# Deformable convolution layer: y offsets of two tap rows loaded onto all lanes, spread matmuls in three batches per row block

## The chip, the core and the metric

The kernel runs on one NeuronCore of a Trainium2 chip. The metric is the device time of one execution in microseconds. Before the change it is 5572.56 us, the median of 3 runs (5569.03 to 5573.76).

## What is computed

Four residual layers act on a 4 x 128 x 128 x 128 image (batch, height, width, channels). Only layer 0 is touched by the change. It is a group norm followed by a deformable 3 x 3 convolution with 4 groups of 32 channels, a ReLU and the residual. Cut to what matters:

```python
offset = einsum('bchw,oc->bohw', gn(x), w_off) + b_off     # 4 groups x 9 taps x (dy, dx)
py = off_y + (ky - 1) + row
px = off_x + (kx - 1) + column
val = bilinear(gn(x), py, px)        # four neighbours, zero outside the image
x = x + relu(einsum('bgckhw,ogck->bohw', val, w_def))
```

Bilinear sampling at (py, px) is the same as summing the pixels q near a place with weights max(0, 1 - |py - qy|) * max(0, 1 - |px - qx|). Each factor is called a tent here. As long as no offset is larger than 1 in size, nine taps around a block of pixels need only a window of pixels around the block; for other inputs a general version stands behind a test at the end of the layer.

## The kernel before, in words

All of it is in `deform_layer` (from L181). The image of each of the 4 batches is cut into 43 blocks of 3 rows (RY = 3), so 172 blocks are worked off in one loop (L699). Inside a block the columns are cut into 33 pieces of 4 columns (RX = 4). A piece of 3 x 4 outputs reads a window of 5 x 6 = 30 pixels; with 4 channel groups these are 120 lanes, the partitions on which most of the work lies.

The stages of a block are these.

1. `load_places` (L444) brings the offsets of a block into `places`: 24 partitions per set (4 groups, 6 parts each), where an offset is kept as three bf16 parts and the three parts of its positive half. Eight transfers on SP's queue per block, from the DRAM tiles `offs`. `load_pixels` (L462) brings the pixel windows, four transfers on SP's queue.
2. `spread_offsets` (L474, matmul L498) turns the offsets of a tap into tents on all 120 lanes with small bf16 matmuls of 25 rows: three of 130 columns for y (one per row of the block) and four of 99 columns for x. Taps are taken in the five slots of `SLOTS` (L50): four slots hold two taps, one holds one. The result lies in `t_ps`, a PSUM tile of two banks in a pool with two buffers.
3. `tents` (L504) multiplies the y tent by the x tent: ACT copies the y part to SBUF (`ty`, L508), DVE multiplies it by the x part in PSUM into `m` (L510). `m` exists twice, for this block and the next.
4. `sample` (L514, matmul L521) multiplies the pixels of a piece, as weights, by `m`, into `v_ps`; ACT copies the result to `v` (`keep_samples`, L528, copy L531).
5. `convolved` (L568, matmul L579) does the 3 x 3 convolution over `v` of this block and the one before, and DVE adds the residual (L552).

The order of the instructions on the five engines is that of the code: L680 asks for a manual schedule. In the loop over the blocks an inner loop of eight steps i (L709) does two things at once: `sample` for four pieces of this block, and the spread and tents of the next block, which `advance` and `DONE` (L650) lay into the steps i = 0, 2, 3, 5 and 6. Between them stand one third of the convolution of the block before, six statistics for the next norm (`count`), and one or two steps of `prepared` (L358), the job that makes the tables of pixels and offsets of later rows: transposes (L370), their copy with the norm (L373), the stores `tab<-rows` (L378, L380), the offset matmul (L385), the offsets (L390, L393), their splitting into parts (L409 to L418) and the store `off<-parts` (L423), once in eight rows.

Each transfer, on whichever queue, takes one of eight completion semaphores in turn. All transfers of the loop are issued by SP.

The loop's inner part, which sets the order on every engine:

```python
for i in range(NG_X):                                    # L709
    if i == 3:
        load_row(n + 2)
    todo = advance(NB_ * (n + 1) + DONE[i])
    if vps is not None:
        keep_samples(*vps)
    next(convs, None)
    vps = sample(m, pix, i, NK * RY), vk, i, NK * RY
    multiply(todo)
```

Of the kernel before, what the change touches and what calls it, by code (L numbers as in the profile page):

```python
# [49 lines left out]
SLOTS = [(0, 6), (1, 7), (2, 8), (3, 5), (4,)]  # L50
# [130 lines left out]
def deform_layer(tc, c, small, x, w_off, b_off, w_def, x1, tabs, offs):  # L181
# [13 lines left out]
    NB = RY * PADW  # L195
    with ExitStack() as ctx:
        wp = ctx.enter_context(tc.tile_pool(name="l0w", bufs=1))
        ps_g = ctx.enter_context(tc.tile_pool(name="l0ps_g", bufs=1, space=PSUM))
        ps_t = ctx.enter_context(tc.tile_pool(name="l0ps_t", bufs=2, space=PSUM))
# [4 lines left out]
        NPH = NPY + NPX  # L204
        keep = ctx.enter_context(tc.tile_pool(name="l0keep", bufs=2))
# [9 lines left out]
        places = [wp.tile([P, len(SLOTS), RY, OW], BF16, name=f"places_{i}") for i in range(3)]  # L215
        last = wp.tile([P, 3, 1, OW], BF16, name="places_last")
        pixels = [wp.tile([P, NXB + 1, P], F32, name=f"pixels_{i}") for i in range(2)]
        parts = wp.tile([2 * NL, NPART, 2 * RO * OW], BF16, name="parts")

        def rims():  # L220

            zero = two.tile([P, 2 * SX * P], F32, name="zero", tag="m")
            nc.vector.memset(zero, 0.0)
            zrow = zero[0 : NXB + 1]
            zoff = zero[0 : 2 * NL, 0 : NPART * OW].bitcast(BF16)
            zoff = zoff.rearrange("p (n l) -> p n l", n=NPART)
            for b in range(B):
# [14 lines left out]
                nc.scalar.dma_start(rows_[:, :, (S + 2) * OW :], zoff)  # L242

        def tables():

            awayi = two.tile([NG, NPH, LANES], I32, name="awayi", tag="x1c")
# [22 lines left out]
            for i, sign in enumerate((-1.0, 1.0, 1.0)):  # L269
                nc.gpsimd.memset(picks[:, i], sign)  # L270
# [17 lines left out]
            for t in (*pixels, parts):  # L288
                nc.gpsimd.memset(t, 0.0)
            yield  # L290
            picks16 = one.tile([NG, 3, P], BF16, name="picks16", tag="ve")
            nc.vector.tensor_copy(picks16, picks.rearrange("g k q r -> g k (q r)"))
            kinds = two.tile([NG, 3, NPH * LANES], BF16, name="kinds", tag="m")
# [10 lines left out]
            n = NPH * LANES // 3  # L304
            for h in range(3):
                if h % 2 == 0:
                    tp = ps_t.tile([P, 2, 512], F32, name="t_ps")
                at = slice(h * n, (h + 1) * n)
                for i in range(3):
                    nc.tensor.matmul(  # L310
                        tp[:, h % 2, 0:n], lhsT=picks16[:, i], rhs=kinds[:, i, at],
                        start=i == 0, stop=i == 2,
                    )
                nc.scalar.copy(to[:, at], tp[:, h % 2, 0:n])
# [43 lines left out]
        def prepared(b, y0):  # L358
# [6 lines left out]
            for h in range(0, RC, RO):  # L365
# [23 lines left out]
                off = one.tile([2 * NL, RO, S], F32, name="off")  # L389
# [8 lines left out]
                p0 = h % (2 * RO)  # L398
                at = slice(p0 * OW, (p0 + RO) * OW)

                def to(i):
                    return parts[:, i, at].rearrange("p (r c) -> p r c", c=OW)[:, :, 2 : S + 2]

                def high(t):
                    halves = t.rearrange("p r c -> p (r c)").bitcast(BF16)
                    return halves.rearrange("p (r c two) -> p r c two", r=RO, two=2)[:, :, :, 1]

                rest = one.tile([2 * NL, RO, S], F32, name="rest")
                nc.scalar.copy(to(0), high(off))  # L409
                nc.gpsimd.tensor_tensor(rest, off, high(off), ALU.subtract)  # L410
                flat = off.rearrange("p r c -> p (r c)")
                nc.vector.tensor_reduce(ranges[:, 0, n : n + 1], flat, AX.X, ALU.max)
                yield
                nc.vector.tensor_reduce(ranges[:, 1, n : n + 1], flat, AX.X, ALU.min)
                nc.scalar.copy(to(1), high(rest))
                nc.gpsimd.tensor_tensor(to(2), rest, high(rest), ALU.subtract)
                yield
                nc.vector.tensor_scalar(  # L418
                    parts[:, NSPLIT:, at], parts[:, 0:NSPLIT, at], 0.0, None, ALU.max
                )  # L420
                if p0:
                    r0 = y0 + h - p0 + 2
                    nc.sync.dma_start(  # L423
                        offs[b].rearrange("(p n) l -> p n l", n=NPART)[
                            :, :, r0 * OW : (r0 + 2 * RO) * OW
                        ],
                        parts,
                    )
                    ready[b] = y0 + h + RO
                    yield  # L430
                yield

        def shifted(b, d, k, n, row, count):

            ky, kx = divmod(k, 3)
            wide = (S + 4) * OW
            first = (d * NK + k) * NG * NPART
            whole = offs[b]
            return bass.AP(
                whole.tensor, whole.offset + first * wide + (row - ky + 2) * OW + 2 - kx,  # L440
                [[wide, NG * NPART], [NG * NPART * wide - 1, n], [1, count]],
            )

        def load_places(b, j):  # L444
            t = places[(b * NYB + j) % 3]
            for d in range(2):
                for q, slot, k, n in ((0, 0, 0, 3), (0, 3, 3, 2), (1, 0, 6, 3), (1, 3, 5, 1)):
                    p1 = 64 * d + 32 * q + 1
                    nc.sync.dma_start(
                        t[p1 : p1 + KROWS - 1, slot : slot + n].rearrange("p k r c -> p k (r c)"),  # L450
                        shifted(b, d, k, n, RY * j, RY * OW),
                    )
            if j + 1 == NYB:
                for d in range(2):
                    p1 = 64 * d + 33
                    nc.sync.dma_start(
                        last[p1 : p1 + KROWS - 1].rearrange("p k r c -> p k (r c)"),
                        shifted(b, d, 6, 3, PADW - 1, OW),
                    )
            return t  # L460
# [13 lines left out]
        def spread_offsets(src, slot, taps, rows):  # L474

            tps, todo = [], []
            for q in taps:
                tp = ps_t.tile([P, 2, 512], F32, name="t_ps")
                tps.append(tp)
                for d in range(2):  # L480
                    p0 = 64 * d + 32 * q
                    wide = OW if d else PADW
                    to = tp[0:LANES, d, 0 : rows * wide].rearrange("p (r c) -> p r c", c=wide)
                    mov = src[p0 : p0 + KROWS, slot]
                    if d == 0:
                        ph0 = 0 if rows == RY else RY
                        lot = [(ph0 + r, to[:, r], mov[:, r, 0:PADW]) for r in range(rows)]
                    else:
                        lot = []
                        for i in range(NPX):  # L490
                            cs = slice(i, OW, RX)
                            lot.append((NPY + i, to[:, :, cs], mov[:, :, cs]))
                    todo.append([(p0, *v) for v in lot])
            for i in range(max(map(len, todo))):
                for lot in todo:
                    if i < len(lot):
                        p0, ph, to, mov = lot[i]
                        nc.tensor.matmul(  # L498
                            to, lhsT=spread[p0 : p0 + KROWS, ph, :], rhs=mov,
                            start=True, stop=True,  # L500
                        )
            return tps

        def tents(tp, m, rows):  # L504

            n = rows * PADW
            ty = two.tile([LANES, NB], F32, name="ty")
            nc.scalar.copy(ty[:, 0:n], tp[0:LANES, 0, 0:n])  # L508
            tx = tp[0:LANES, 1, 0 : rows * OW].rearrange("p (r c) -> p r c", c=OW)[:, :, 0:PADW]
            nc.vector.tensor_tensor(  # L510
                m, ty[:, 0:n].rearrange("p (r c) -> p r c", c=PADW), tx, ALU.mult
            )
# [55 lines left out]
        def convolved(b, y0, y1, terms, stats, first, each):  # L568
# [7 lines left out]
            for m, ((ky, at, v, k0, r0, r1), kx) in enumerate(todo):  # L576
                if m >= first and (m - first) % each == 0:
# [3 lines left out]
                    rhs=v[:, k0 + kx, r0:r1, kx : kx + S],  # L581
# [66 lines left out]

        NB_ = len(SLOTS)
        DONE = [1, 1, 2, 3, 3, 4, 5, 5]  # L650
        assert len(DONE) == NG_X and DONE[-1] == NB_
        rows_in, ms = {}, {}
        made = [0]

        def advance(upto):

            todo = []
            while made[0] < min(upto, NB_ * len(blocks)):
                n, slot = divmod(made[0], NB_)
                taps = range(len(SLOTS[slot]))  # L660
                tps = spread_offsets(rows_in[n], slot, taps, RY)
                todo.extend((n, SLOTS[slot][q], tp) for q, tp in zip(taps, tps))
                made[0] += 1
            return todo

        def multiply(todo):
            for n, k, tp in todo:
                if n not in ms:
                    ms[n] = two.tile([LANES, NK, RY, PADW], F32, name="m")
                tents(tp, ms[n][:, k], RY)  # L670
# [7 lines left out]

        order = {getattr(mybir.EngineType, e) for e in ("PE", "Activation", "DVE", "Pool", "SP")}
        ctx.enter_context(tc.manual_schedule(engines=order))  # L680
        nc.scalar.dma_start(woff, w_off)
        nc.scalar.dma_start(boff, b_off.rearrange("o n -> n o"))
# [13 lines left out]
        for i in range(NB_):  # L696
            multiply(advance(i + 1))
# [1192 lines left out]
```

## Time and profile before

| what | value |
|---|---|
| median of the runs | 5572.56 us |
| the profiled execution, and its span | 5567.76 us, 5565.9 us |
| mean granted TensorE clock | 0.971 |
| PE busy in the span | 5163.0 us (93%) |
| DVE, ACT, POOL busy | 3079.9 (55%), 2721.1 (49%), 787.0 us (14%) |
| first and last sample matmul of the loop | 119.0 us, about 3304 us |
| SP's queue: packets, MB, share of 16 DMA engines | 1127664, 657.77, 45.2% |
| ACT's queue: packets, MB, share | 10182, 6.43, 0.4% |
| spread matmuls L498 | x10836 on `places`, x60 on `places_last` |
| sample matmuls L521 | x11352 on `m`, x264 on `me` |

The profile is of one execution. Busy time counts instructions at work, without waits; a group's line gives the busy time, the mean duration of one instruction, and the idle time of the engine before it with what ended it. Matmuls are pipelined, so their durations overlap; what one costs the engine is read from the starts of the timeline. The granted clock is the share of full speed that the throttle gave TensorE. The DMA share is the mean over the core's sixteen DMA engines.

### The profile page before, as it was taken

The numbers are of one execution on the slowest core, as the hardware profiler recorded it, in microseconds if no ns is written. First come the engines' busy times: TensorE is split into PE (matmuls) and PEld (weight loads), VectorE is DVE, ScalarE is ACT, GpSimd is POOL, SyncE is SP. The second block draws the span as 40 slices with busy tenths as digits, with TensorE's granted clock in tenths as the row PEclk, the third lists the DMA queues.
The fourth block names the chain that finished last, engine by engine and source line by source line (L and its number), as shares of the span: only waits on it lengthen the run. The fifth ranks groups of instructions, "written<-read, shape, count | busy, mean of one in ns | idle before, by whom it ended". The sixth has DMA issues, their size and how long they took to land. (4 is left out here: it accounts for less than half of the span.)

```text
span 5565.9 us, 112097 instructions
## 1 busy us (share of the span) xinstructions
PE 5163.0 (93%) x42401; PEld 4438.1 (80%) x42401; DVE 3079.9 (55%) x10450; ACT 2721.1 (49%) x5802; POOL 787.0 (14%) x698
## 2 busy tenths in 40 slices
PE   2899999999999999999999989999989889898896
PEld 1778888888888888888888878999967768577686
DVE  6544444554444644444433337888876574764844
ACT  1345555445554455554544432333345475664755
POOL 2021111001111011111100002222210010110102
PEclk9899999999999999999999989999989999999999
DMA  4555555555555555554543423233232352642525
GB/s 142 146 129 137 128 136 122 127 118 135 133 131 119 131 112 137 129 141 113 124 78 76 76 56 91 91 107 103 91 100 92 97 195 80 207 147 82 203 95 169
DMA packets 1138394, 671.46 MB, mean 121 GB/s; under 512 B 737133, under 2 KB 1003566, under 8 KB 1121206
## 3 DMA queue, kind: packets, MB, share of 16 engines
q1 hardware_dynamic: 1127664, 657.77, 45.2%
q8 instruction: 338, 5.54, 0.4%
q10 hardware_dynamic: 10182, 6.43, 0.4%
q14 instruction: 210, 1.72, 0.1%
HBM read 382.88 MB, written 281.11 MB: 119 GB/s over the span
## 5 line engine op out<-in xcount | busy, mean ns | idle before, releaser
L510 DVE TENSOR_TENSOR m<-ty,t_ps 120x390 f32<-120x390 f32 x1548 | 805.0, 557 | 1497.2 <-ACT ty L508 1496.0
L521 PEld LDWEIGHTS v_ps<-m,pixels 120*128 120x128 f32 x11352 | 1436.1, 194 | 86.0 <-issue 8.7
L521 PE MATMUL v_ps<-m,pixels 120*128 120x108 f32 (+1 forms) x11352 | 1462.3, 273 | 3.6 <-ACT v L531 3.5
L531 ACT COPY v<-v_ps 128x432 f32<-128x432 f32 x1376 | 719.7, 523 | 1268.7 <-PE v_ps L521 1265.8
L579 PE MATMUL conv_ps<-v,wdef 128*128 128x128 f32 (+2 forms) x5160 | 1301.8, 378 | 6.5 <-DVE x1c L552 5.9
L579 PEld LDWEIGHTS conv_ps<-v,wdef 128*128 128x128 f32 x5160 | 812.8, 192 | 256.0 <-issue 21.7
L508 ACT COPY ty<-t_ps 120x390 f32<-120x390 f32 x1560 | 688.2, 489 | 176.9 <-PE t_ps L498 169.5
L498 PE MATMUL t_ps<-places,spread 25*120 25x99 bf16 (+1 forms) x10836 | 520.0, 259 | 62.1 <-DVE m L510 37.8
L498 PEld LDWEIGHTS <-spread 25*120 25x120 bf16 x10896 | 338.9, 136 | 224.5 <-issue 124.6
L1639 PEld LDWEIGHTS proj_ps<-wcat,X 128*128 128x128 f32 x4096 | 473.2, 192 | 19.1 <-issue 18.9
L393 POOL TENSOR_TENSOR off<-off,koff 72x512 f32<-72x512 f32 x128 | 162.1, 1266 | 2294.1 <-DVE off L390 2215.8
L1639 PE MATMUL proj_ps<-wcat,X 128*128 128x128 f32 x4096 | 481.3, 276 | 0.0
L1072 ACT ACTIVATE rowT<-x1T_ps,t_x,s_x 128x128 f32<-128x128 f32 x512 | 192.7, 457 | 366.4 <-PE x1T_ps L1065 342.8
L1085 PE MATMUL m_ps<-carry,w 128*128 128x172 f32 x2286 | 361.5, 311 | 0.0
L1646 DVE TENSOR_TENSOR L<-proj_ps,work 128x256 f32<-128x256 f32 x256 | 108.6, 424 | 430.0 <-ACT work L1643 429.9
L1085 PEld LDWEIGHTS m_ps<-carry,w 128*128 128x128 f32 x2286 | 345.5, 188 | 0.0
L1185 POOL TENSOR_TENSOR sum_h<-sum_h,x2c 128x512 f32<-128x512 f32 x128 | 163.2, 1275 | 1159.4 <-DVE x2c L1145 1159.4
L1736 POOL TENSOR_TENSOR gate<-normed,gate 128x512 f32<-128x512 f32 x128 | 163.4, 1276 | 1127.8 <-ACT normed L1735 867.2
L1643 ACT ACTIVATE work<-proj_ps 128x512 f32<-128x512 f32 x256 | 152.1, 598 | 293.2 <-PE proj_ps L1639 287.8
L1746 PE MATMUL out_ps<-outw,gate 128*128 128x128 f32 x1024 | 190.2, 288 | 30.3 <-POOL gate L1736 30.3
L1746 PEld LDWEIGHTS out_ps<-outw,gate 128*128 128x128 f32 x1024 | 162.9, 200 | 38.9 <-POOL gate L1736 38.9
L1449 PE MATMUL self_ps<-R,ws 128*128 128x512 f32 x256 | 147.3, 680 | 32.4 <-DVE X L1460 17.3
(237 smaller groups left out, 6499.6 us busy)
## 6 DMA issues: line engine op xcount, KB each, us to landing
pixels<-tab SPq DMA_DIRECT2D x688, 123.8 KB
xin<-in_x_dram SPq DMA_DIRECT2D x56, 1024.0 KB
off<-parts SPq DMA_DIRECT2D x64, 891.0 KB
tab<-rows SPq DMA_DIRECT2D x384, 128.0 KB
places<-off SPq DMA_DIRECT2D x688, 55.7 KB
x<-x1c SPq DMA_DIRECT2D x32, 1024.0 KB
x1rows<-x SPq DMA_DIRECT2D x128, 256.0 KB
x2T<-x2c SPq DMA_DIRECT2D x128, 256.0 KB
```

Of the source, the lines that this page charges most:

```text
L498: nc.tensor.matmul(to, lhsT=spread[p0 : p0 + KROWS, ph, :], rhs=mov, start=True, stop=True,)
L508: nc.scalar.copy(ty[:, 0:n], tp[0:LANES, 0, 0:n])
L510: nc.vector.tensor_tensor(m, ty[:, 0:n].rearrange("p (r c) -> p r c", c=PADW), tx, ALU.mult)
L521: nc.tensor.matmul(vp[:, h * n : h * n + rows * w].rearrange("p (k c) -> p k c", c=w), lhsT=pix[0:LANES, xb, :], rhs=m[:, :, RX * xb : RX ...
L531: nc.scalar.copy(v[:, :, c0 : c0 + 4 * RX].rearrange("p k (h c) -> p k h c", c=RX), vp[:, 0 : 4 * n].rearrange("p (h k c) -> p k h c", h=4 ...
L579: nc.tensor.matmul(pc[:, at : at + r1 - r0, :], lhsT=wdef[:, 3 * ky + kx, :], rhs=v[:, k0 + kx, r0:r1, kx : kx + S], start=m == 0, stop=m ...
L1072: nc.scalar.activation(rt[:, b, :], px[:, b, :], AF.Identity, bias=t, scale=s)
L1085: nc.tensor.matmul(to, lhsT=wgt, rhs=src[:, :, at : at + n], start=i == 0, stop=i + 1 == len(todo),)
L1185: nc.gpsimd.tensor_tensor(sum_h, sum_h, x2c[:, :, i], add)
L1639: nc.tensor.matmul(pp[:, j], lhsT=X[:, j0 + j, :], rhs=wcat[:, cols], start=True, stop=True)
L1736: nc.gpsimd.tensor_tensor(gt, a, gt, ALU.mult)
L1746: nc.tensor.matmul(po[:, j], lhsT=a[:, j], rhs=outw, start=False, stop=True)
```

## The change

The channels of the offset layer are put into another order (the weights are loaded in pieces), so that the y offsets of the first two rows of taps (ky = 0 and 1; six of nine taps) come first: NLY = 24 of 72 channels. In `prepared` these go in f32 from the tile `offwide` to new DRAM tiles `offys`, in three stores per four rows, each shifted by its kx. The other 48 channels go as parts to `offs`, now every four rows instead of every eight.

`load_places` now issues two transfers on ACT's queue and four on SP's (before: eight on SP's). The two bring, for ky = 0 and 1, 3 rows x 3 taps x 132 columns (4752 bytes) of f32 onto each of the 120 lanes; the 30 lanes of a group read the same data. They land in `tent`, a ring of three tiles that takes the place of `m`. ACT makes |offset + lane's distance| there in place (`across`, three instructions per block), and DVE makes min(|.| - 1, 0) of it (`lowered`, one instruction per block).

The spread matmuls remain for all x offsets and for the y offsets of ky = 2. They are done in three batches of 15, one per kx, at i = 2, 4 and 6, each in one PSUM tile of four banks with a single buffer. `tents` then has one ACT copy and two DVE products per batch: one over the two loaded rows, in place, and one for ky = 2. The layout of `v` changes with it (ky, row, kx), and `places` has two buffers instead of three.

```diff
-        ps_t = ctx.enter_context(tc.tile_pool(name="l0ps_t", bufs=2, space=PSUM))
+        ps_t = ctx.enter_context(tc.tile_pool(name="l0ps_t", bufs=1, space=PSUM))
...
+        wide = wp.tile([2 * NL, RO, OW + 2], F32, name="offwide")
+        tent = [wp.tile([LANES, KS, RY, KS, OW], F32, name=f"tent_{i}") for i in range(3)]
...
+                r0 = y0 + h + 2
+                for kx in range(KS):
+                    nc.sync.dma_start(
+                        offys[b][:, r0 : r0 + RO, kx, :],
+                        wide[2 * NG * kx : 2 * NG * (kx + 1), :, 2 - kx : 2 - kx + OW],
+                    )
...
+        def same_on_lanes(b, ky, row):
+
+            whole = offys[b]
+            return bass.AP(
+                whole.tensor,
+                whole.offset + (ky * NG * (S + 4) + row - ky + 2) * KS * OW,
+                [[(S + 4) * KS * OW, NG], [0, NS], [1, RY * KS * OW]],
+            )
+
         def load_places(b, j):
-            t = places[(b * NYB + j) % 3]
...
+            t = places[(b * NYB + j) % 2]
+            y = tent[(b * NYB + j) % 3]
+            from_ = [(X0 + KS * NG * NPART * ky, ky) for ky in range(KS)] + [(0, KS - 1)]
+            for q, (first, ky) in enumerate(from_):
+                if q < KS - 1:
+                    nc.scalar.dma_start(
+                        y[:, q].rearrange("p r k c -> p (r k c)"), same_on_lanes(b, q, RY * j)
+                    )
+                nc.sync.dma_start(
+                    t[32 * q + 1 : 32 * q + KROWS].rearrange("p k r c -> p k (r c)"),
+                    shifted(b, first, ky, RY * j, RY * OW),
+                )
...
+        def spread_offsets(src, rows, taps):
+
+            tp = ps_t.tile([P, KS + 1, 512], F32, name="t_ps")
+            ph0 = 0 if rows == RY else RY
+            for i in range(NPX):
+                cs = slice(i, OW, RX)
+                for q in (*taps, KS):
+                    at = slice(32 * q, 32 * q + KROWS)
+                    to = tp[0:LANES, q, 0 : rows * OW].rearrange("p (r c) -> p r c", c=OW)
+                    if q < KS:
                         nc.tensor.matmul(
+                            to[:, :, cs], lhsT=spread[at, NPY + i, :], rhs=src[at, :, cs],
                             start=True, stop=True,
                         )
+                    elif i < rows:
+                        nc.tensor.matmul(
+                            to[:, i], lhsT=spread[at, ph0 + i, :], rhs=src[at, i],
+                            start=True, stop=True,
+                        )
+            return tp
+
+        def across(n, r):
+            t = tent[n % 3][:, 0 : KS - 1, r].rearrange("p k x c -> p k (x c)")
+            nc.scalar.activation(t, t, AF.Abs, bias=lane_y[:, r : r + 1])
+
+        def lowered(n):
+            t = tent[n % 3][:, 0 : KS - 1]
+            nc.vector.tensor_scalar(t, t, 1.0, 0.0, ALU.subtract, ALU.min)
+
+        def tents(tp, m, loaded, rows):
+
+            n = rows * OW
+            ty = two.tile([LANES, RY * OW], F32, name="ty")
+            nc.scalar.copy(ty[:, 0:n], tp[0:LANES, KS, 0:n])
+            tx = tp[0:LANES, 0:KS, 0:n].rearrange("p k (r c) -> p k r c", c=OW)
+            if loaded is not None:
+                nc.vector.tensor_tensor(loaded, loaded, tx[:, 0 : KS - 1], ALU.mult)
             nc.vector.tensor_tensor(
+                m, ty[:, 0:n].rearrange("p (r c) -> p r c", c=OW), tx[:, KS - 1], ALU.mult
             )
...
             for i in range(NG_X):
-                if i == 3:
+                if i == 1:
                     load_row(n + 2)
-                todo = advance(NB_ * (n + 1) + DONE[i])
+                kx = i // 2 - 1
+                batch = more and i in (2, 4, 6)
+                if batch:
+                    tp = spread_row(n + 1, kx)
                 if vps is not None:
                     keep_samples(*vps)
                 next(convs, None)
                 vps = sample(m, pix, i, NK * RY), vk, i, NK * RY
-                multiply(todo)
...
+                if more and i < 2:
+                    for r in range(i, 2 * i + 1):
+                        across(n + 1, r)
+                if more and i == 1:
+                    lowered(n + 1)
+                if batch:
+                    multiply(n + 1, kx, tp)
```

## The prediction

> **What bounds the kernel now.** I read the busy time by stage first. The two stretches below are the whole sampling loop (first sample matmul at 119.0 us, last at about 3304) and its steady middle; the columns are length, then busy us of PE, PEld, DVE, ACT, POOL, then granted clock, DMA share and GB/s.
>
> ```profile
> core 0: us, PE busy (x) PEld busy (x) DVE busy (x) ACT busy (x) POOL busy (x), PEclk, DMA share, GB/s
> 119.00:3304.00 3185.00, 3124.45 (x28377) 2633.90 (x28377) 1480.51 (x4266) 1611.00 (x3519) 420.83 (x378) 0.98 0.53 119
> 1100.00:2300.00 1200.00, 1186.97 (x10859) 999.55 (x10857) 602.06 (x1850) 620.06 (x1348) 170.39 (x153) 0.99 0.56 128
> ```
>
> PE is busy 1187 of 1200 us at a granted 0.99, DVE and ACT half the time, the DMA engines 0.56. The loop is 4 x 43 = 172 blocks, so one block takes 3185 / 172 = 18.5 us, and PE sets it. The change touches this loop and a few us of setup; the 2260 us behind it stay.
>
> Second, PE's timeline over one block (start, length, engine, line, operation):
>
> ```profile
> 1503.62 0.56 PE L498 MATMUL t_ps<-places,spread 25*120 25x130 bf16 x14
> 1504.11 0.71 PE L579 MATMUL conv_ps<-v,wdef 128*128 128x128 f32 x4
> 1504.65 1.04 PE L521 MATMUL v_ps<-m,pixels 120*128 120x108 f32 x8
> 1506.43 0.29 PE L498 MATMUL t_ps<-places,spread 25*120 25x130 bf16 x2 [0.73 <-DVE m L510]
> 1506.90 0.55 PE L498 MATMUL t_ps<-places,spread 25*120 25x130 bf16 x12 [0.17 <-DVE m L510]
> ...
> 1514.17 0.55 PE L498 MATMUL t_ps<-places,spread 25*120 25x130 bf16 x7
> 1514.65 1.13 PE L579 MATMUL conv_ps<-v,wdef 128*128 128x256 f32 x4
> ```
>
> Starts, not lengths, give the price: a two-tap batch of 14 spread matmuls holds PE for 1504.11 - 1503.62 = 0.49 us, and a one-tap batch of 7 for 0.48. The matmuls on different 32-row groups overlap; a batch costs its longest group, four matmuls, whatever stands beside it. The 0.73 and 0.17 are PE waiting for DVE to free t_ps.
>
> Third, the groups by line with shapes kept apart, for ACT's and DVE's prices (busy, mean ns | idle before):
>
> ```profile
> L510 DVE TENSOR_TENSOR m<-ty,t_ps 120x390 f32<-120x390 f32 x1548 | 805.0, 557 | 1497.2 <-ACT ty L508 1496.0
> L531 ACT COPY v<-v_ps 128x432 f32<-128x432 f32 x1376 | 719.7, 523 | 1268.7 <-PE v_ps L521 1265.8
> L508 ACT COPY ty<-t_ps 120x390 f32<-120x390 f32 x1548 | 685.0, 491 | 159.1 <-PE t_ps L498 151.6
> ```
>
> Both engines mostly wait for PE. Fourth, the DMA issues, because the new loads are large:
>
> ```profile
> pixels<-tab SPq DMA_DIRECT2D x688, 123.8 KB
> off<-parts SPq DMA_DIRECT2D x64, 891.0 KB
> places<-off SPq DMA_DIRECT2D x688, 55.7 KB
> ```
>
> **The change on PE: a gain.** Five spread batches a block become three. Each new one has 12 x-matmuls of 99 columns in three row groups and 3 y-matmuls of 132 in a fourth: four in the longest group again, so 0.49 us. Saved: 2 x 0.49 = 0.98 us a block. The batches now stand two sample steps apart instead of one, so the waits for DVE at the spread (37.8 + 3.4 us in the list of waits) should go: 0.24 a block. If nothing else moved: 18.5 - 1.2 = 17.3 us a block, 210 us less.
>
> **ACT.** Out go 9 ty copies, 685 / 172 = 4.0 us a block. In come 3 copies (1.5); three Abs passes over 792 values with a per-partition bias (the activation with bias on 512 takes 719 ns, with scale and bias on 128 457 ns; extended, about 0.95 each, 2.9); and two DMA issues. An issue from ACT took 0.35 us for wdef and 0.8 for the zeros of off, so 0.7 to 1.6 for both. Sum 5.1 to 6.0, so 1 to 2 us more on an engine that has 9 idle.
>
> **DVE.** Out: 4.7 us. In: one tensor_scalar over 2376 f32 (512 values take 538 ns and 128 take 338, so 0.52 ns each: 1.5 us); three products of 792 (390 values 557 ns, 130 values 291 ns, so 0.97 each) and three of 396 (0.56). Sum 6.1, 1.4 us more on an engine half idle.
>
> **Their order decides.** t_ps has one buffer now, so the spread at i = 4 waits until DVE has multiplied the batch of i = 2. From the block's first sample, PE reaches that spread after 1526.83 - 0.67 - 1520.40 = 5.8 us (the second batch there taken out). The other way: keep_samples starts at 1.1 and ends at 1.6, two Abs passes to 3.5, lowered to 5.0, products to 6.5, or 7.2 where a range reduction (0.68) falls between. PE waits 0.8 to 1.5 us there, more if the issues ahead of that keep_samples are slow. Behind the waiting lowered stand DVE's statistics; behind ACT's waits stand keep_samples and ty. So this new wait alone gives back about what PE saved: 17.3 becomes 18.1 to 18.8, up to 19.5 with slow issues.
>
> **DMA, which I take to be the new bound.** Each block adds two loads of 120 pieces of 4752 bytes. Medians of the trace's packets in the loop: 128 bytes 13 ns, 792 38 ns, 8192 312 ns; 4096-byte packets elsewhere 159. On that line 4752 bytes take about 183 ns (an estimate). 240 pieces are 43.9 us of one engine, 2.7 us a block if all sixteen share: nothing, under 0.6 busy. How many share? The records of SP's queue contain 51,920 four-byte packets, the completion marks. Of SP's 3650 transfers 1384 touch 24 partitions, 688 touch 30, 64 (off) run from 72 partitions to 432 lines, 1514 have sizes divisible by 16. 1384 x 12 + 688 x 15 + 64 x 12 + 1514 x 16 = 51,920 exactly; sixteen marks each would be 58,400. This is the rule of the Trainium skill, "DMA: Bandwidth & Descriptors", section "Why a DMA increments its semaphore by 16 and not by 1": a transfer runs on the largest number of engines, at most 16, that divides the slowest dimension of both sides, and those are the lowest-numbered ones. The new load's source is [4 groups][30 repeats][1188] against 120 partitions: 4 engines, and by the page the same four for both. That no trace of before shows a transfer on four is the risk.
>
> On those four a block then holds: tents 60 x 183 ns = 11.0 us. The rest, by medians: pixels 264 x 13 = 3.4, places 24 x 38 = 0.9 (was 1.4), table rows 1.0, x tiles 1.3, residual rows 0.6, off and offy 0.8, marks 0.1: 8.1. Together 19.1. The loop's mean packet is longer than the median (the share 0.53 x 18.5 = 9.7 us instead of 8.1); with everything stretched so, about 22.9. By an even spread the same sum is 8.1 + 2.7 = 10.8. So four engines need 19.1 to 22.9 us a block, above the 18.1 to 18.8 of PE's and DVE's way. I take the middle, 21.0. The eight completion semaphores, which the built program gives in turn to the transfers of SP and ACT, carry the lag on: the tents' issue on ACT waits for the transfer eight before it, and the next pixels and places wait for the tents.
>
> Edits I cost at nothing: the three offy stores per four rows and off stored every four rows (SP issues of 0.3 to 0.85 us, in the gaps of its queue, against four places loads fewer; without that cover under 1 us a block); wide, read by the offy stores, rewritten a whole step round later; eight small setup loads and eight zero stores on ACT (up to 6 us, under the statistics that last to 77 us); places with two buffers, read out a block before reuse.
>
> **Sum.** (21.0 - 18.5) x 172 = 430 us more. The profiled execution took 5567.76 (span 5565.9), giving 5998; the median of the runs is 5 us higher: about 6000.
>
> **Rivals and chances** (0.2% is what a measurement of this kernel can tell).
> Four engines bound the loop, 19.7 to 22.9 us a block: 5780 to 6320, likeliest 6000; chance 0.71.
> Worse: with the four saturated, ACT also stands in its issues or waits for semaphores, and its stall adds to DVE's chain (1 to 2 us more on 22.5): 6400 to 6600; 0.09. For it: SP's pixel issues take 0.65 us where 0.32 is the least. Against: 60 descriptors are few.
> The tents spread wider or overlap the small packets, and the t_ps chain bounds: 18.8 to 19.5 us, 5620 to 5740; 0.11.
> The other side: the tents spread over eight engines or more (5.5 us each at eight, 13.6 in all, below 17.3), and DVE's chain ends within the 5.8 us, 0.8 us sooner than laid out above. Then PE's two batches count: 17.3 to 18.2 us, 5360 to 5520, say 5400; 0.07. It decides once an engine's share falls under 17 us.
> No change by cancellation: 0.02.
> Faster 0.07, same 0.02, slower 0.91. The range 5690 to 6330 holds the first case and half of the third; outside stay about 0.19.
>
> **What would show it.** Right: PE's busy share in the loop falls to 0.80 to 0.88; waits name the tent loads, ACT's Abs or its queue, or pixels; the L498 group becomes 45 matmuls a block with batches of 0.49 us; the first packets of a tent load to its last span 8 us or more; blocks of about 21 us. The wait at the i = 4 spread on DVE shows the chain. Wrong: tents landing in 3 to 4 us, PE still over 0.97 busy, and lowered far from 1.5 us would each break a step.

## The result and the profile after

The changed kernel takes 6965.98 us, the median of 4 runs (6952.06 to 6976.43); the kernel before took 5570.8 (5566.38 to 5573.76). The ratio is 1.2504 [1.248, 1.2528]: 1395 us more. The direction was forecast; the size, 430 us, was not, and the range ended at 6330.

First the busy time by stage, the view that the prediction began with. The columns are length, then busy us of PE, PEld, DVE, ACT and POOL, then granted clock, DMA share and GB/s; the first row spans the whole loop, the second the same steady middle as before.

```profile
core 0: us, PE busy (x) PEld busy (x) DVE busy (x) ACT busy (x) POOL busy (x), PEclk, DMA share, GB/s
119.00:4700.00 4581.00, 3328.36 (x25336) 2798.43 (x25331) 1648.75 (x3928) 1607.90 (x3008) 412.95 (x378) 0.83 0.47 119
1100.00:2300.00 1200.00, 871.81 (x6668) 734.18 (x6668) 448.24 (x1135) 424.93 (x795) 110.34 (x102) 0.84 0.48 122
```

PE is busy 872 of 1200 us (before 1187) at a granted 0.84 (before 0.99). The DMA share has even fallen, from 0.56 to 0.48. The sample matmuls on `tent` start from 131.9 to 4684.9 us, so a block takes 4553 / 172 = 26.5 us instead of 18.4 (those on `m` before, counted in the same way). This 8.0 us, times 172, is 1381 us; the later start of the loop is 13 more. All the loss is in the loop.

The groups of PE, ACT and DVE (page of the changed kernel; busy, mean ns | idle before) show that the computation itself costs what it should:

```profile
L557 PE MATMUL v_ps<-tent,pixels 120*128 120x108 f32 (+1 forms) x11352 | 1620.0, 293 | 204.1 <-ACT v L567 174.6
L615 PE MATMUL conv_ps<-v,wdef 128*128 128x128 f32 (+2 forms) x5160 | 1476.4, 418 | 320.8 <-DVE x1c L588 319.0
...
L545 DVE TENSOR_TENSOR tent<-tent,t_ps 120x792 f32<-120x792 f32 x516 | 502.8, 974 | 1080.5 <-ACT ty L542 1073.5
L536 DVE TENSOR_SCALAR tent<-tent 120x2376 f32<-120x2376 f32 x172 | 240.3, 1397 | 845.8 <-ACT tent L532 845.8
...
L532 ACT ACTIVATE tent<-tent,lane_y 120x792 f32<-120x792 f32 x516 | 475.2, 955 | 29.1 <-DMA tent<-offy 28.9
...
L546 DVE TENSOR_TENSOR tent<-ty,t_ps 120x396 f32<-120x396 f32 x516 | 288.0, 558 | 0.0
```

0.96 us for an Abs pass, 1.40 for `lowered`, 0.97 and 0.56 for the products. What is new is in the idle columns, and in the first two rows: the same 11352 and 5160 matmuls that were busy 1462.3 and 1301.8 us before are busy 1620.0 and 1476.4, 332 us more, on the lower clock. Their two lines before were

```profile
L521 PE MATMUL v_ps<-m,pixels 120*128 120x108 f32 (+1 forms) x11352 | 1462.3, 273 | 3.6 <-ACT v L531 3.5
...
L579 PE MATMUL conv_ps<-v,wdef 128*128 128x128 f32 (+2 forms) x5160 | 1301.8, 378 | 6.5 <-DVE x1c L552 5.9
```

The list of waits of the changed kernel (us in total, times, longest) names who was late. Before, the wait at the spread for DVE came to 37.8 us, and each of the other five, at the same places, to under 8 us:

```profile
ACT parts L430 <- DMA off<-parts: 549.9, 76, 16.4
...
DVE x1c L588 <- DMA xres<-in_x_dram: 344.3, 80, 20.4
...
PE conv_ps L615 <- DVE x1c L588: 340.9, 111, 18.9
...
PE t_ps L519 <- DVE tent L546: 240.9, 106, 11.6
PE img_ps L392 <- DMA xin<-in_x_dram: 234.6, 26, 20.1
...
PE v_ps L557 <- ACT v L567: 174.6, 62, 14.0
```

Hardly anybody waits long for a tent load by name (ACT 28.9 us). They wait for `xres`, `xin` and `off`: other transfers, all of SP's. The waits of SP's own queue say why:

```profile
SPq L434 <- DMA tent<-offy: 576.8, 68, 23.3
...
SPq L500 <- DMA tent<-offy: 401.7, 61, 12.8
...
SPq L484 <- DMA tent<-offy: 238.2, 33, 17.2
...
SPq L400 <- DMA tent<-offy: 177.9, 19, 18.1
```

With the smaller lines of this kind SP stands 1596 us until a tent load has landed, although no instruction of SP uses a tent: SP's next transfer is to use a completion semaphore that the load still holds. Before there is no such line.

SP also stands inside its issues. The list by tile (minimum, median and maximum ns of one issue) has for the pixels

```profile
L500 SPq DMA_DIRECT2D pixels<-tab x688: 315/708/14781, 115.3 to 4656.7; - x172
```

where the longest issue before took 4548 ns. Summed from the records up to the last sample matmul, SP's issues last 2305 us (before 1720), with 1281 us for the pixels (before 631). Of the pixel issues 157 last over 2 us, 896 us together; in 90% of this time packets of the tents are in flight, in the whole loop in 56%.

How this reaches PE is seen in the timeline (start, length, engine, line, operation; a row of SP is from the start of the first of xN issues to the end of the last, standing included):

```profile
1508.59 3.60 SPq L609 DMA_DIRECT2D xres<-in_x_dram  x1
...
1513.26 0.61 ACTq L481 DMA_DIRECT2D tent<-offy  x1
...
1513.98 0.36 SPq L352 DMA_DIRECT2D xin<-in_x_dram  x1
1514.43 0.63 ACTq L481 DMA_DIRECT2D tent<-offy  x1
1514.74 19.70 SPq L500 DMA_DIRECT2D pixels<-tab  x4
1525.80 1.11 DVE L356 BATCH_NORM_STATS2 stats<-xin 128x6 f32<-128x64 f32 x8 [18.44 <-DMA xin<-in_x_dram]
...
1529.80 1.65 PE L615 MATMUL conv_ps<-v,wdef 128*128 128x256 f32 x3 [16.67 <-DVE x1c L588]
```

The four pixel issues, 0.7 us each by the median, take 19.70 us beside the two tent loads of ACT. `xin`, issued between the tent loads, lands after 11.8 us. DVE's statistics stand for it, `x1c` is queued behind them, and PE pauses 16.67 us.

### The profile page after: what moved, and what is told of

Read it like the earlier page. It is cut to its first block, busy times and chain, and to the rows that moved or that the text cites. A ratio compares the mean times of both kernels' runs of the same rounds, so it can differ in the third digit from the quotient of the medians.

```text
span 6962.8 us, 105522 instructions
## 1 busy us (share of the span) xinstructions
PE 5356.9 (77%) x39311; PEld 4598.4 (66%) x39311; DVE 3239.1 (47%) x10107; ACT 2715.7 (39%) x5286; POOL 775.5 (11%) x702
## 5 line engine op out<-in xcount | busy, mean ns | idle before, releaser
L557 PEld LDWEIGHTS v_ps<-tent,pixels 120*128 120x128 f32 x11352 | 1600.0, 212 | 332.6 <-ACT v L567 194.0
L557 PE MATMUL v_ps<-tent,pixels 120*128 120x108 f32 (+1 forms) x11352 | 1620.0, 293 | 204.1 <-ACT v L567 174.6
L615 PE MATMUL conv_ps<-v,wdef 128*128 128x128 f32 (+2 forms) x5160 | 1476.4, 418 | 320.8 <-DVE x1c L588 319.0
L545 DVE TENSOR_TENSOR tent<-tent,t_ps 120x792 f32<-120x792 f32 x516 | 502.8, 974 | 1080.5 <-ACT ty L542 1073.5
L536 DVE TENSOR_SCALAR tent<-tent 120x2376 f32<-120x2376 f32 x172 | 240.3, 1397 | 845.8 <-ACT tent L532 845.8
L519 PE MATMUL t_ps<-places,spread 25*120 25x99 bf16 x6192 | 331.1, 301 | 326.9 <-DVE tent L546 231.3
L415 POOL TENSOR_TENSOR offwide<-offwide,koff 72x512 f32<-72x512 f32 x128 | 154.2, 1205 | 3508.2 <-DVE offwide L412 3436.9
L532 ACT ACTIVATE tent<-tent,lane_y 120x792 f32<-120x792 f32 x516 | 475.2, 955 | 29.1 <-DMA tent<-offy 28.9
L542 ACT COPY ty<-t_ps 120x396 f32<-120x396 f32 (+1 forms) x528 | 255.3, 483 | 476.6 <-PE t_ps L519 322.1
L546 DVE TENSOR_TENSOR tent<-ty,t_ps 120x396 f32<-120x396 f32 x516 | 288.0, 558 | 0.0
```

The lines of the kernel that those rows point to most:

```text
L519: nc.tensor.matmul(to[:, :, cs], lhsT=spread[at, NPY + i, :], rhs=src[at, :, cs], start=True, stop=True,)
L532: nc.scalar.activation(t, t, AF.Abs, bias=lane_y[:, r : r + 1])
L536: nc.vector.tensor_scalar(t, t, 1.0, 0.0, ALU.subtract, ALU.min)
L542: nc.scalar.copy(ty[:, 0:n], tp[0:LANES, KS, 0:n])
L545: nc.vector.tensor_tensor(loaded, loaded, tx[:, 0 : KS - 1], ALU.mult)
L546: nc.vector.tensor_tensor(m, ty[:, 0:n].rearrange("p (r c) -> p r c", c=OW), tx[:, KS - 1], ALU.mult)
```

## The experiments

Each ratio is to the kernel before on the same chip (5571.57 to 5575.72 us).

**Twelve engines instead of four.** Three copies of each row of `offys` in DRAM, so that the source's slowest dimension has 12 entries (NC = 3, and three times the stores of `offys`).

```diff
-                [[(S + 4) * KS * OW, NG], [0, NS], [1, RY * KS * OW]],
+                [[(S + 4) * KS * OW, NG * NC], [0, NS // NC], [1, RY * KS * OW]],
```

> The y offsets stand three times in DRAM, so that a tent load reads from 12 slow-dimension entries instead of 4 and, by the rule of the prediction, runs on twelve engines. Same bytes onto the lanes; SP issues nine small stores per four rows instead of three. Theory FOUR FULL (the four DMA engines are simply full, a block lasts as long as their work) and theory QUEUE (the long landing of the two loads keeps the eight shared semaphores and so the issue of all other transfers waiting, while the four engines are not full): both expect a landing of 3 to 4 us instead of 8, and 18 to 19.5 us a block, 5450 to 5800 us. Theory CHAIN (not the transfers, but the single t_ps buffer with ACT's and DVE's longer chain): about 6900 us, no change.

6305.13 us, 1.1312 [1.1286, 1.1338]. The packets of one load now take 3.4 us from the first to the last (median of the records) instead of 7.2, and it lands 7.1 us after its issue instead of 14.1; the second load of a block stands behind the first. The width is real and worth 661 us, but more than half of the loss stays, 798 us over no loads; both theories expected at most some 290.

**Half the columns, four engines.** The loads bring 594 of 1188 values per lane; the rest of the tents is wrong.

```diff
-                [[(S + 4) * KS * OW, NG], [0, NS], [1, RY * KS * OW]],
+                [[(S + 4) * KS * OW, NG], [0, NS], [1, RY * KS * OW // 2]],
```

> The two loads stay on four engines, but bring only the first half of the columns (594 of 1188 values per lane); the other half of each tile keeps what stood there, so the tents are not the layer's. FOUR FULL: the four engines' work falls to 13.6 to 16 us a block, under PE's own 17.3, so the time falls all the way to that of the kernel without loads, within 1%. QUEUE: each load still lands after 4 us, so part of the waits of SP stays: clearly slower than without loads, 5800 to 6300 us. CHAIN: about 6900 us.

6094.23 us, 1.0931 [1.0912, 1.095]. Half the bytes still cost 587 us over no loads. By the prediction's own sum four engines would need 11.0 / 2 + 8.1 = 13.6 us a block here, up to 16 with the longer packets, under PE's 18; were full engines the only bound, nothing would be left.

**No loads.** Only the first three blocks load; the tents of later blocks are made from old data.

```diff
-                if q < KS - 1:
+                if q < KS - 1 and b * NYB + j < 3:
```

> The tent loads are issued for the first three blocks only; afterwards Abs, min and the products work on what is left in the tiles, so the output is not the layer's. All other instructions stay. FOUR FULL and QUEUE: the rest of the change alone, PE's saving against the t_ps chain: 17.5 to 19.0 us a block, 5400 to 5660 us. CHAIN: about 6900 us.

5507.2 us, 0.9882 [0.9865, 0.9899]: a small gain of 1.2%. In the steady middle PE is busy 1140 of 1200 us and the clock is back at 0.99:

```profile
1100.00:2300.00 1200.00, 1139.71 (x10027) 969.95 (x10026) 668.64 (x1662) 639.04 (x1192) 169.02 (x156) 0.99 0.54 119
```

Its block takes 3090 / 172 = 18.0 us. So the rest of the change is worth -66 us, and the two loads alone 1459 us.

**The loads apart.** The second load of a block moves from i = 1 to i = 3.

```diff
-                if q < KS - 1:
+                if q < 1:
...
+                if i == 3 and n + 2 < len(blocks):
+                    load_second(*blocks[n + 2])
```

> Both loads on four engines and in full, but the second one is issued two steps later (i = 3 instead of i = 1). FOUR FULL: the same work on the four engines, so the same time within 2%, 6830 to 7100 us. QUEUE: only one long load holds semaphores at a time and other transfers get in between, so 6300 to 6750 us. CHAIN: no change.

6833.04 us, 1.2274 [1.2246, 1.2302]: 133 us less, no more. This lies just within the range of FOUR FULL (6830 to 7100) and above that of QUEUE (6300 to 6750). The bunching is a small part.

**Issued by POOL**, whose transfers have semaphores of their own; with four entries, then with twelve.

```diff
-                    nc.scalar.dma_start(
+                    nc.gpsimd.dma_start(
```

> The two tent loads as in the change (four slow-dimension entries), but issued by POOL, whose transfers take semaphores of their own, so that SP's transfers no longer wait for a tent load eight places before them. Bytes and number of transfers stay. FOUR FULL: the four engines keep their work, 6700 to 7000 us. QUEUE (the shared eight semaphores): most of the 1460 us over the version without loads goes, 5600 to 6000 us.

> Issued by POOL and read from twelve entries (three copies in DRAM). FOUR FULL: about e1_twelve, 6305 us, since only the queue differs. QUEUE: near the version without loads, 5500 to 5650 us. If POOL's own issue of a load is slow, a few tens of us more by POOL's delay of the offsets.

6293.13 us, 1.1271 [1.1242, 1.1299], and 5894.94 us, 1.0565 [1.0547, 1.0582]. SP now waits for no tent load by semaphore, yet both end above what QUEUE expected, by 293 and 245 us, and below what FOUR FULL did. With four entries SP's pixel issues last 1583 us in sum. So the semaphores are one way in which SP comes to stand behind the tents; a longer issue is another. Nor is this pair clean. The queues on the two pages (packets, MB, share of 16 engines) show quite different numbers of packets: first with four entries,

```profile
q0 software_dynamic: 170624, 196.68, 13.6%
```

then with twelve,

```profile
q0 software_dynamic: 60544, 196.24, 14.1%
```

The pieces of 4752 bytes are 120 a load in both; the rest are packets of four bytes, 376 and 56 a load. And with four entries most often eight packets of the tents are in flight at once (39% of the time that any is), where ACT's loads had four (70%): POOL's two loads run beside each other, not one behind the other.

**The tents made a block earlier.** Abs and `lowered` move to i = 5 to 7 of the block before, so that nothing waits for them; first with no loads (the tents again from old data), then complete, with POOL and twelve entries.

```diff
-                if more and i == 1:
-                    lowered(n + 1)
+                if n + 2 < len(blocks) and i >= 5:
+                    across(n + 2, i - 5)
+                if n + 2 < len(blocks) and i == 7:
+                    lowered(n + 2)
```

> No tent loads after the third block (output not the layer's), and Abs and min of a block are done a block earlier, in steps 5 to 7, so that they no longer stand between the first sample and the spread of step 4. If the chain into the single t_ps took 0.8 us a block in the version without loads (18.1 instead of 17.3), its time falls to 5340 to 5420 us. If not the chain, but slower batches or ACT took it: 5490 to 5520 us, no change.

> Complete kernel: loads by POOL from twelve entries, Abs and min a block earlier. If queue and chain are the two costs: 5350 to 5500 us, faster than the kernel before. If the landing of the loads is late for the earlier Abs (under 9 us left): as e6_pool_twelve or slower.

Without loads 5431.73 us, 0.9743 [0.9726, 0.9759], just above the expected 5340 to 5420: the chain of one `t_ps` costs 75 us, 0.44 us a block. With loads 5881.21 us, 1.056 [1.0531, 1.0589], hardly less than the 5894.94 without the move. There ACT waits for the loads (10.6 us without the move):

```profile
ACT tent L534 <- DMA tent<-offy: 242.7, 84, 14.3
```

**Issued by SP, four entries.** The same transfers, in program order before the places that stand next to them.

```diff
-                    nc.scalar.dma_start(
+                    nc.sync.dma_start(
```

> The two tent loads on four engines issued by SP instead of ACT; they take the same eight shared semaphores. If the loads cost through these semaphores and the four engines: as the changed kernel within 2%, 6830 to 7100 us. If ACT's issuing (two issues of 0.62 us a block, and ACT standing in them) was part of it, at least 100 us less: under 6830.

6470.7 us, 1.1617 [1.1596, 1.1638]: 495 us less than from ACT. My first expectation was no difference; my reason for the second, that ACT stands in its issues, does not fit either, since none of them took over 1.15 us in the changed kernel. On ACT, a tent load is issued a median 20.7 us before SP reaches the places next to it in the code; here it is 0.7 us (from the starts of the issues). SP waits for tents 639 us instead of 1596, and its pixel issues last 777 us instead of 1281. Now the late load shows under its own name:

```profile
ACT tent L532 <- DMA tent<-offy: 666.6, 127, 12.9
```

**Tiny loads.** 66 of 1188 values, from ACT, four entries; the rest of the tents is wrong.

```diff
+                [[(S + 4) * KS * OW, NG], [0, NS], [1, 66]],
```

> The two loads as in the change, but 66 of 1188 values per lane (264 bytes a piece), so that they land in about 2 us; number of transfers, issues and waits stay (the tents are not the layer's). If only the length of the landing counts: 5500 to 5600 us, the version without loads. If two more transfers in the turn of eight, or their issue, cost by themselves: 5700 us or more.

5626.92 us, 1.0098 [1.0081, 1.0115]: 120 us over no loads, between the two expectations; a load lands after 2.6 us (median). Two more transfers a block cost little by themselves: 1339 of the 1459 us go with their length.

**The kernel before, with loads that nobody reads.** Two loads of 960 values per lane from x, 81% of the bytes of the tents, and `places` with two buffers; first ACT with four entries, then POOL with twelve. Nothing of the changed computation is in it.

```diff
+        extra = wp.tile([LANES, 2, 960], F32, name="extra")
...
+                nc.scalar.dma_start(
+                    extra[:, q],
+                    bass.AP(
+                        x.tensor,
+                        x.offset + (q * 12 + b) * 16384 + 384 * (j % 32),
+                        [[16384, 4], [0, LANES // 4], [1, 960]],
+                    ),
+                )
```

> The kernel before with nothing of the change but two loads per block of 960 values onto each of 120 lanes, four slow-dimension entries, issued by ACT into a tile that nobody reads (81% of the change's bytes; places has two buffers to make room). If the loads alone make the loss: 5573 plus about 1100, 6450 to 6900 us. If it takes the change's other parts too (t_ps with one buffer, the longer chain): under 6200 us.

> The same addition to the kernel before, issued by POOL and read from twelve entries. By the difference of e6_pool_twelve and e3_no_loads (388 us) and 81% of the bytes: 5780 to 5960 us. If that rest came from the change's other parts: 5573 to 5700 us.

6728.46 us, 1.2076 [1.2056, 1.2096], and 5870.09 us, 1.0532 [1.0515, 1.055], both as expected. Loads alone make the loss: the first stands 1157 us above the kernel before, against 1395 us for the complete change. There SP's queue shows the same wait for a tile that no instruction reads, 2060 us in sum; its largest line is

```profile
SPq L462 <- DMA extra<-in_x_dram: 1619.4, 253, 13.6
```

**SP and twelve entries together.**

> Loads issued by SP, in program order with its other transfers, and read from twelve entries. If width and order are separate costs: by the pairs e1_twelve (661 less) and e9_sp_issue (495 less), with part of each shared as on POOL, 5850 to 6050 us. If both are the same cost seen twice (the late landing), about e1_twelve: 6200 to 6350 us.

5805.86 us, 1.0418 [1.0401, 1.0436], a little under the expected range. On SP and ACT the two remedies add up:

| loads | four entries | twelve entries | saved |
|---|---|---|---|
| issued by ACT | 6966 | 6305 | 661 |
| issued by SP | 6471 | 5806 | 665 |
| issued by POOL | 6293 | 5895 | 398 |
| saved, ACT to SP | 495 | 499 | |

In its steady middle PE is at 1083 of 1200 us and a clock of 0.94:

```profile
1100.00:2300.00 1200.00, 1083.17 (x9077) 916.95 (x9077) 627.42 (x1729) 570.93 (x1066) 135.37 (x123) 0.94 0.73 169
```

**Both loads later.** The whole `load_row` back at i = 3, from ACT with four entries.

```diff
-                if i == 1:
+                if i == 3:
```

> The change with the whole load of a row (both tent loads and places) two steps later, at i = 3 instead of i = 1, still on ACT and four engines. If ACT's running ahead of SP by some 21 us is the cost that SP's issue removes: two steps of some 3 us take only part of it away, 6650 to 6900 us. If the order does not matter: 6900 to 7050 us. If the loads then land too late for Abs: over 7050 us.

6794.88 us, 1.2188 [1.2168, 1.2209]: 171 us less, as expected. A tent load is now issued 16.1 us ahead instead of 20.7. No complete version beats the kernel before. The 5432 us of the early tents without loads would need the loads for nothing.

What connects the runs is how long SP stands. For each run with the computation in its place I summed from the records what SP's issues last beyond those without loads (SP's own tent issues and additional stores taken out), and its waits for tents:

| run | issues longer, us | waits for tents, us | sum | time over no loads, us |
|---|---|---|---|---|
| changed kernel | 825 | 1596 | 2421 | 1459 |
| twelve | 328 | 1169 | 1497 | 798 |
| apart | 941 | 1324 | 2265 | 1326 |
| both later | 662 | 1648 | 2310 | 1288 |
| half | 272 | 1203 | 1475 | 587 |
| POOL, four | 1360 | 0 | 1360 | 786 |
| SP, four | 363 | 639 | 1002 | 964 |
| POOL, twelve | 775 | 0 | 775 | 388 |
| SP, twelve | 126 | 282 | 408 | 299 |
| tiny | 0 | 668 | 668 | 120 |

Where ACT or POOL issues full or half loads, 40 to 60% of what SP stands reaches the time; the rest is hidden by its slack. With tiny loads it is 18%. Where SP issues the loads itself, it is 73 and 96%: there the tents themselves come late as well. The table connects; it is not a proof of the share.

## Why the prediction was wrong in its size

The step that failed is the pricing of the loads: "So four engines need 19.1 to 22.9 us a block, above the 18.1 to 18.8 of PE's and DVE's way. I take the middle, 21.0." It set the block equal to the work of four full engines. Two things were off in it.

The smaller is the size of that work. A packet of a tent takes 220 ns in the mean of the loop; the sum used 183, near the median of 184. With the mean, four engines have 60 x 0.220 = 13.2 us of tents a block and 9.2 us of all other packets (an estimate, the others spread evenly over sixteen), 22.4 us together. This is close to the upper end, 22.9, not to the middle.

The larger is the time in which these engines had no work, for which the sum has no term: the block took 26.5 us, 4.1 more. Between 1100 and 2300 us no packet at all was in flight in 11.7% of the time (from the packets' records). With half the bytes the same estimate gives 16.0 us, under PE's 18, and the block took 21.5. Where this time comes from is the order: long loads issued 21 us ahead of their turn, and SP standing behind them. When SP issued the same loads in its own order, the estimate gives 22.9 of 23.5 us a block, and no packet was in flight in only 3.4% of the time. There the four engines are nearly full, as the step had it. So the mechanism that the prediction named is there, and the order comes on top of it: of 1459 us over no loads, 964 remain with SP's order on four engines and 798 with ACT's on twelve.

The sentence that held this, that the eight completion semaphores "carry the lag on", was given no price. Issuing the loads in SP's order instead of ACT's saves 495 us on four engines and 499 on twelve, which is more than the whole forecast loss. The eight entries shared by two queues and the loads' place ahead of the pixels change together there. The hardware queue changes with them too, so how the engines share their time between two queues is a third possibility that no run separates. POOL, with semaphores of its own, also ran ahead, and SP then stood in its issues. So the 495 us go with the order of issue; how much of them belongs to the semaphores alone is not settled.

**Where the 8.5 us a block over the kernel without loads are.** In the steady middle PE's pauses over 1 us sum to 312 us (stretches in which neither a matmul nor a weight load runs, from the records) in 1200 / 26.5 = 45.3 blocks, 6.9 us a block; without loads it is 40 us in 66.8 blocks, 0.6. The sample and convolution matmuls are 1620.0 + 1476.4 - 1461.0 - 1292.4 = 343 us busier, 2.0 a block. So 18.0 + 6.3 + 2.0 = 26.3 of 26.5. The prediction had no term for the clock. The two lines without loads are

```profile
L557 PE MATMUL v_ps<-tent,pixels 120*128 120x108 f32 (+1 forms) x11352 | 1461.0, 275 | 16.0 <-DMA pixels<-tab 9.9
L615 PE MATMUL conv_ps<-v,wdef 128*128 128x128 f32 (+2 forms) x5160 | 1292.4, 376 | 35.5 <-DVE x1c L588 33.5
```

The other steps:

- **Four engines of sixteen: right.** On average 3.6 packets of the tents are in flight while any is, and the semaphore's records show four single completion marks at the end of each load, twelve with twelve entries. Here the Trainium skill's rule ("DMA: Bandwidth & Descriptors", "Why a DMA increments its semaphore by 16 and not by 1") held, and twelve entries saved 661 and 665 us.
- **Batches of 15 matmuls in 0.49 us: right.** The timeline of the changed kernel shows two of them up to the next convolution:

```profile
1499.90 0.30 PE L519 MATMUL t_ps<-places,spread 25*120 25x99 bf16 x3
...
1500.38 0.71 PE L615 MATMUL conv_ps<-v,wdef 128*128 128x128 f32 x4
...
1504.73 0.30 PE L519 MATMUL t_ps<-places,spread 25*120 25x99 bf16 x3 [1.42 <-DVE tent L546]
...
1505.22 1.56 PE L615 MATMUL conv_ps<-v,wdef 128*128 128x384 f32 x4
```

- **ACT, DVE: right.** The two issues cost 1.2 us a block (0.616 each; 0.7 to 1.6 forecast), the new instructions as forecast.
- **The chain of one `t_ps`: right in kind, too dear.** The 1.42 above is it; over the loop it is 0.44 us a block instead of 0.8 to 1.5. The kernel without loads runs at 18.0 us a block, just under the forecast 18.1 to 18.8. PE's saving, forecast at 1.2 us, comes to 0.9: from 18.4 to 18.0, and the 0.44.
- **The worse rival** (6400 to 6600 us, chance 0.09) had the mechanism half right: an issuer that stands. It was SP, in 1281 us of pixel issues, and not ACT, whose 344 issues never took over 1.15 us. The argument against it, "60 descriptors are few", held for ACT's own issues; it left out those of SP behind them.
- **"Tents landing in 3 to 4 us" and "PE still over 0.97 busy"** did not show; the wait at the spread on DVE did (240.9 us). PE's busy share fell to 0.73, below the 0.80 to 0.88 that was to show the prediction right, and the waits name `xres`, `xin` and `off` rather than the tents.

Open is the last 299 us of the best placed loads (SP, twelve) over none: their bytes, the six additional stores per four rows that the copies need, and tents that land late were not separated.

## What to carry to other kernels

A transfer's price is more than bytes over engines: count how many engines it runs on, price its packets by the mean of a loaded loop and not by the median, and then ask which other transfers come behind it, on those engines and on the semaphores that the queues share. A load moved to another engine's queue can run far ahead of its turn, and what then stands is not the reader of the load but the queue with everything else. To learn whether an added transfer or an added computation makes a loss, put the transfer alone, unread, into the old kernel.

## What the runs showed of the hardware that was not expected

- TensorE's granted clock followed the pauses. Without loads PE made no pause over 3.4 us in the steady middle and had 0.99. With them it made 27 such pauses, 232 us in all, and had 0.84; SP with twelve entries had 6 (28 us) and 0.94. The Trainium skill ("TensorE: Matmul & The Clock Gate", "What's actually happening") lets the clock fall to half after an idle window of about 3.4 us. The two values agree, since the records of the changed kernel hold no others than 1.0 and 0.5; the window does so only in part. In these 1200 us the changed kernel has 45 stretches at 0.5 against the 27 pauses, and the kernel without loads has four (27 us) although its longest pause is 3.15 us. So shorter pauses go with the lower clock too. The waits of a transfer so cost PE twice: here 6.3 us a block in pauses and 2.0 in slower matmuls.
- An issue on SP can last up to 14.8 us (median 0.7) in a kernel where another queue's long loads are in flight, and the issues over 2 us stand nearly all beside such loads (90% of their time). Why the issue stands is not shown. The list of waits does not name it: it is found in the duration of the issue.
- A load of 120 pieces from POOL leaves 496 packets with a source of four entries (170624 / 344) and 176 with one of twelve (60544 / 344) for the same 120 pieces: the difference is packets of four bytes, 376 against 56.
